# A smaller ordering margin, summed weights for a node's own messages, and two full matmuls for the targets' terms

## The chip, the cores and the metric

The kernel runs on one core of one Trainium2 chip. The metric is the device time of one execution in microseconds; the time before is the median of three runs, 4530.78 us (4525.29 to 4530.98). A profile is one more execution with the hardware profiler on. Engines are called PE (TensorE matmul), PEld (its weight loads), DVE (VectorE), ACT (ScalarE), POOL (GpSimd) and SP (which issues the DMAs).

## The reference

64 graphs of 256 nodes with 128 features pass through four residual graph layers (a graph convolution, a hyperbolic one, one with messages per edge, and a four-step dense one). All is fp32. The adjacency matrices are sparse: about 3% of the entries beside the diagonal are not zero, and the diagonal is full. The change touches only layer 2, whose core is:

```python
m_j = einsum('bnd,do->bno', node_features, W1[:D])      # sources
m_i = einsum('bnd,do->bno', node_features, W1[D:])      # targets
pre = m_j[:, None, :, :] + m_i[:, :, None, :] + b1
msg = gelu(layernorm(pre, g1, be1))                     # exact
agg = einsum('bijo,bij->bio', msg, adjacency)
updated = layernorm(concat([node_features, agg]) @ W2 + b2, g2, be2)
```

A message from a node to itself has both terms from the same node: `h @ W1[:D] + h @ W1[D:] + b1`. That equals `h @ (W1[:D] + W1[D:]) + b1`.

## The kernel before, in words

**Edges in lanes.** A graph's adjacency is cut into 8 blocks of 32 targets by 3 blocks of 86 sources, 24 blocks. The edges of a block (without the diagonal) are packed into 128 lanes. `g.hot` holds for each block a matrix with two ones for every lane: one at the row of its source (rows 0 to 85) and one at the row of its target (rows 96 to 127). One matmul of `hot` with a `table` that has the sources' terms in rows 0 to 85 and the targets' terms in rows 96 to 127 therefore gives the sum of both for all lanes of the block.

**Layer 2** (line 1039). After a layer norm, a ReLU and a transpose, `hT` (features by nodes, 128x256) is the input of four pieces which run side by side (`together`, line 1101):

- `sources` (line 1057): three matmuls with `w1[:, 0, :]` into one PSUM bank, the bias added by DVE into `a`, then four copies on POOL into `table[:86]`, two for the first four target blocks and two for the rest.
- `targets(0)` and `targets(1)` (line 1086): each makes four matmuls, one for 32 targets, all with output partitions 96 to 127 of a bank of its own, waits in the plan until the previous graph has left the stage of messages, and has ACT copy the bank, repeated for three source blocks, into `table[96:, c*4:(c+1)*4]`.
- `diagonal` (line 1046): for each half of the nodes two accumulating matmuls with the two parts of `w1` give the own messages' terms, DVE adds the bias into `mown`, and `messages` (line 1017) makes norm and GELU of them.

Then come six blocks of messages (`block_sums`, line 1106): four `table,hot` matmuls into a bank of the pool `psm`, squares on ACT (`junk`, with the sum in `sq`), a reciprocal root on POOL (`sq`), scale on DVE (`msg`), an offset on POOL, the GELU on ACT, and four matmuls into `pagg`, whose four outputs lie in four groups of 32 partitions. There is one `table` and one `pagg`, so a graph can fill the table only when the one before has left this stage.

**PSUM.** Five banks (`ps`) serve nearly everything, two (`psm`) the message blocks, one is `pagg`.

**Order.** Each layer of each graph is a generator that issues an instruction or a few and yields. `run` (line 1228) keeps several graphs alive and decides who goes next. A planner (`Clock`, line 60) adds an assumed duration to every issued instruction, knows when each engine and each tile will be free, and so gives each live generator a time at which its next instruction could begin. Of those whose time lies within a margin of the earliest, the one with the lowest graph number is taken. The order so found is kept word for word (`keep_in_program_order`, line 177, the line under which nearly all instructions appear in the profile), and each engine works through its part of it in order. A change of an assumed duration, of the number of pieces or of the margin therefore moves instructions of the whole program. The planner counts a matmul with an output of at most 32 columns of weights as a quarter of a full one.

**ACT's function tables.** Exp and Ln need one table, GELU and Tanh another; the planner puts an `ACT_TABLE_LOAD` (line 106) wherever its order changes between them.

Of the kernel before, what the change touches and what calls it, by code (L numbers as in the profile page):

```python
# [10 lines left out]
ALU = mybir.AluOpType  # L11
# [4 lines left out]
P = 128  # L16
N = 256
NC = N // P
D = 128
# [7 lines left out]
CAP = 128  # L27
TB = 4
TE = 6
MSGS = 4  # L30

LN_EPS = 1e-5
# [149 lines left out]
class Sparse:  # L182
# [142 lines left out]
    def setup(self):  # L325
        nc, w = self.nc, self.w
        self.ident = self.c("ident", [P, P])
        make_identity(nc, self.ident)
        self.ones = self.full("ones", [P, P], 1.0)
        self.half = self.full("half", [P, 2 * NC], 0.5)  # L330
        self.mhalf = self.full("mhalf", [P, NT], -0.5)

        self.w0 = self.matrix("w0", w["L0_gnn_W"])
        self.b0 = self.row("b0", w["L0_gnn_b"])

        self.attw = self.c("attw", [P, 2])
        self.column(None, w["L1_gnn_att_w"][D : 2 * D], self.attw[:, 0:1])
        self.column(None, w["L1_gnn_att_w"][0:D], self.attw[:, 1:2])
        self.attb = self.row("attb", w["L1_gnn_att_b"])

        self.w1 = self.matrix("w1", w["L2_gnn_W1"])
        wsum = self.c("wsum", [P, 2])
        nc.vector.tensor_reduce(wsum, self.w1, AX.X, ALU.add)
        nc.vector.tensor_scalar_mul(wsum, wsum, 1.0 / D)
        for k in range(2):
            nc.vector.tensor_scalar(self.w1[:, k, :], self.w1[:, k, :], wsum[:, k : k + 1], None, ALU.subtract)
        self.b1 = self.row("b1", w["L2_gnn_b1"])
        bsum = self.c("bsum", [P, 1])  # L350
        nc.vector.tensor_reduce(bsum, self.b1, AX.X, ALU.add)
        nc.vector.tensor_scalar_mul(bsum, bsum, -1.0 / D)
        nc.vector.tensor_scalar(self.b1, self.b1, bsum[:, 0:1], None, ALU.add)

        self.g1 = self.row("g1", w["L2_gnn_g1"])
        nc.vector.tensor_scalar_mul(self.g1, self.g1, float(D) ** 0.5)
        self.be1 = self.row("be1", w["L2_gnn_be1"])
        self.w2 = self.matrix("w2", w["L2_gnn_W2"])
        self.b2 = self.row("b2", w["L2_gnn_b2"])
        self.g2 = self.row("g2", w["L2_gnn_g2"])  # L360
        self.be2 = self.row("be2", w["L2_gnn_be2"])
        self.setup_layer3()
        self.setup_lanes()
# [675 lines left out]
    def layer2(self, n, g):  # L1039
# [6 lines left out]
        def diagonal():  # L1046
            po = yield from self.bank(self.ps, (P, NC, D))
            for c in range(NC):
                self.mm(po[:, c, :], [(hT[:, c * P : (c + 1) * P], self.w1[:, k, :]) for k in range(2)])
            yield  # L1050
            nc.vector.tensor_tensor(own, po, self.over(self.b1, NC), ALU.add)
            yield
            self.close(self.ps)
            yield
            yield from self.messages(own, own, NC)

        def sources():

            pa = yield from self.bank(self.ps, (P, NJB, D))
            for j in range(NJB):  # L1060
                w = self.width(j)
                self.mm(pa[:w, j, :], [(hT[:, j * JB : j * JB + w], self.w1[:, 0, :])])
            yield
            a = self.t("a", [P, NJB, D], bufs=1)
            w = self.width(NJB - 1)
            b1 = self.over(self.b1, NJB)
            nc.vector.tensor_tensor(a[:JB, : NJB - 1], pa[:JB, : NJB - 1], b1[:JB, : NJB - 1], ALU.add)
            yield
            nc.vector.tensor_tensor(a[:w, NJB - 1], pa[:w, NJB - 1], self.b1[:w], ALU.add)
            yield  # L1070
            self.close(self.ps)
            while self.left["messages"] < n:
                yield
            self.clock.since(self.when.get(("messages", n - 1), 0.0))
            yield
            for c in range(NC):
                rows = slice(c * NQ, (c + 1) * NQ)
                for js, k in ((slice(0, NJB - 1), JB), (slice(NJB - 1, NJB), w)):
                    near = a[:k, js].rearrange("p (o j) d -> p o (j d)", o=1)
                    nc.gpsimd.tensor_copy(  # L1080
                        table[:k, rows, js].rearrange("p i j d -> p i (j d)"),
                        near.to_broadcast([k, NQ, near.shape[2]]),
                    )
                    yield

        def targets(c):
            pc = yield from self.bank(self.ps, (P, NQ, D))
            for q in range(NQ):
                i = c * NQ + q
                self.mm(pc[P - IB :, q, :], [(hT[:, i * IB : (i + 1) * IB], self.w1[:, 1, :])])  # L1090
            yield
            while self.left["messages"] < n:
                yield
            self.clock.since(self.when.get(("messages", n - 1), 0.0))
            far = pc[P - IB :].rearrange("p q (o d) -> p q o d", o=1).to_broadcast([IB, NQ, NJB, D])
            nc.scalar.copy(table[P - IB :, c * NQ : (c + 1) * NQ], far)
            yield
            self.close(self.ps)
            yield

        yield from self.together(n, [sources(), targets(0), targets(1), diagonal()])
        yield from self.enter(n, "layer2", "messages")
        g.sums = 0
        pagg = self.psa.tile([P, NC, D], F32, tag="pagg", name="pagg")
# [123 lines left out]
    def run(self, x, adj, out, B):  # L1228


        def point(one):

            at = []
            while hasattr(one, "gi_frame") and one.gi_frame:
                at.append((one.gi_code.co_name, one.gi_frame.f_lineno))
                one = one.gi_yieldfrom
            return tuple(at)

        first = {}
        layers = {  # L1240
            "load": (lambda n, g: self.load(n, g, x, adj, out), "load"),
            "adjacency": (self.adjacency, "adjacency"),
            "scaled": (self.scaled, "scaled"),
            "layer0": (self.layer0, "layer0"),
            "lanes": (self.lanes, "hot"),
            "layer1": (self.layer1, "map"),
            "layer2": (self.layer2, "update"),
            "layer3": (self.layer3, "end"),
        }

        self.behind = {
            "load": [("pairs", 5), ("scaled", 5), ("layer0", 2)],
            "adjacency": [("load", 0), ("layer0", 2), ("scaled", 3)],
            "scaled": [("adjacency", 0), ("end", 2)],
            "layer0": [("adjacency", 0), ("map", 3)],
            "lanes": [("load", 0), ("ball", 3)],
            "hot": [("messages", 3)],
            "layer1": [("layer0", 0), ("pairs", 2), ("map", 3)],
            "pairs": [("hot", 0), ("messages", 3)],
            "ball": [],  # L1260
            "map": [("update", 3)],
            "layer2": [("map", 0), ("update", 2)],
            "messages": [],
            "update": [("end", 2)],
            "layer3": [("update", 0), ("scaled", 0)],
            "end": [],
        }
        graphs = [Graph() for _ in range(B)]
        clock = self.clock
        self.left = dict.fromkeys(self.behind, 0)  # L1270
        self.when = {}
        begun = dict.fromkeys(layers, 0)
        live = self.live = []
        while self.left["end"] < B:
            for name, (layer, last) in layers.items():
                n = begun[name]
                if n < B and self.ready(n, name):
                    live.append([self.at(n, name), n, name, layer(n, graphs[n]), last])
                    begun[name] += 1

            points = [point(one[3]) for one in live]
            begin = [max(one[0], clock.free.get(first.get(p), 0.0)) for one, p in zip(live, points)]
            soon = min(begin) + 0.2
            k = min((k for k in range(len(live)) if begin[k] <= soon), key=lambda k: (live[k][1], begin[k]))
            one = live[k]
            clock.now = clock.end = one[0]
            clock.first = None
            over = next(one[3], live) is live
            if clock.first:
                first[points[k]] = clock.first  # L1290
            one[0] = max(clock.end, one[0] + 0.1)
            if over:
                clock.end = one[0]
                live.remove(one)
                if one[4]:
                    self.leave(one[1], one[4])
# [614 lines left out]
```

## Time and profile before

| what | value |
|---|---|
| median of three runs | 4530.78 us |
| the profiled execution | 4534.37 us, of which the span from first to last instruction is 4532.6 |
| mean granted PE clock | 0.838 of full speed |
| ACT_TABLE_LOAD | 376 loads, 482.4 us of ACT, 1283 ns each |
| DVE `hot<-bank,lane` | 512 instructions, 266.5 us |
| POOL `ersn<-ew,mhalf` (a power of 24 columns) | 64 instructions, 271.1 us, 4236 ns each |

The page gives each engine's busy time and its share of the span, the span in 40 slices, the chain of work that ended last (followed back from the last instruction, at each step to what released it) and the costliest groups of instructions. A group is written as `output<-inputs`, its shape, its count, its busy time, the mean of one in ns, and the engine's idle time just before it with what ended that. All PSUM banks are called `bank`; the weights `w0`, `w1` and `w2` all appear as `w`. A matmul's shape `128*32 128x128` means 128 rows by 32 columns of weights and a moving operand of 128 by 128. Over the 64 graphs the span gives about 71 us a graph, while a graph is under way for several times as long: three to four are in the program at any time.

### The profile page before, as it was taken

The numbers are of one execution on the slowest core, as the hardware profiler recorded it, in microseconds if no ns is written. First come the engines' busy times: TensorE is split into PE (matmuls) and PEld (weight loads), VectorE is DVE, ScalarE is ACT, GpSimd is POOL, SyncE is SP. The second block draws the span as 40 slices with busy tenths as digits, with TensorE's granted clock in tenths as the row PEclk, the third lists the DMA queues.
The fourth block names the chain that finished last, engine by engine and source line by source line (L and its number), as shares of the span: only waits on it lengthen the run. The fifth ranks groups of instructions, "written<-read, shape, count | busy, mean of one in ns | idle before, by whom it ended". The sixth has DMA issues, their size and how long they took to land.

```text
span 4532.6 us, 85967 instructions
## 1 busy us (share of the span) xinstructions
PE 3624.9 (80%) x29143; PEld 3001.5 (66%) x29143; DVE 3154.1 (70%) x11739; ACT 2441.3 (54%) x7801; POOL 2831.3 (62%) x4945
## 2 busy tenths in 40 slices
PE   6688888778878878888787867888688888787876
PEld 5567666666767666666676656677576766676664
DVE  8666776677767767877676767767677677767652
ACT  2546555455556555655455455565555565655542
POOL 3666666576566666666566575665666666666653
PEclk7788878888888888888898878888887888888887
DMA  1000000000000000000000000000000000000000
GB/s 47 6 7 9 7 10 9 10 7 9 7 11 10 7 10 9 7 11 10 6 11 9 10 6 10 7 9 10 7 9 7 9 7 10 10 9 7 3 3 4
DMA packets 61585, 42.16 MB, mean 9 GB/s; under 512 B 6096, under 2 KB 61136, under 8 KB 61136
## 3 DMA queue, kind: packets, MB, share of 16 engines
q1 hardware_dynamic: 61136, 36.59, 2.9%
q8 instruction: 231, 3.78, 0.3%
q14 instruction: 218, 1.79, 0.1%
HBM read 28.19 MB, written 8.39 MB: 8 GB/s over the span
## 4 chain that ended last, share of the span: by engine, by line
PE 41%; DVE 24%; POOL 21%; ACT 8%; issue 5%; DMA 0%; SPq 0%; POOLq 0%; DVEq 0%; ACTq 0%
PE bank L177 40%; POOL sq L177 5%; POOL msg L177 4%; DVE msg L177 3%; POOL ersn L177 3%; POOL lnrs L177 2%; DVE hot L177 2%; ACT junk L177 2%; ACT L106 2%; DVE agg L177 2%; DVE src L177 1%; PE pagg L177 1%; DVE x2o L177 1%; DVE lnst L177 1%; ACT msg L177 1%
## 5 line engine op out<-in xcount | busy, mean ns | idle before, releaser
L177 DVE SCALAR_TENSOR_TENSOR msg<-bank,sq,g 128x128 f32<-128x128 f32 x1536 | 449.0, 343 | 271.7 <-POOL sq L177 256.9
L177 POOL TENSOR_TENSOR msg<-msg,be 128x512 f32<-128x512 f32 x384 | 490.3, 1281 | 173.2 <-DVE msg L177 134.9
L177 PE MATMUL bank<-table,hot 128*128 128x128 f32 x3072 | 459.4, 300 | 133.8 <-DVE msg L177 124.7
L177 PEld LDWEIGHTS bank<-table,hot 128*128 128x128 f32 x3072 | 420.9, 210 | 175.5 <-issue 49.7
L177 ACT ACTIVATE junk<-bank 128x128 f32<-128x128 f32 x1536 | 409.2, 278 | 189.9 <-PE bank L177 187.8
L106 ACT ACT_TABLE_LOAD x376 | 482.4, 1283 | 6.6
L177 POOL TENSOR_TENSOR sq<-sq,mhalf 128x4 f32<-128x4 f32 (+1 forms) x448 | 449.1, 1002 | 37.3
L177 PE MATMUL bank<-entries,hot 128*128 128x69 f32 x3072 | 443.8, 307 | 7.6 <-ACT entries L177 5.2
L177 PEld LDWEIGHTS bank<-entries,hot 128*128 128x128 f32 x3072 | 433.7, 224 | 24.4 <-issue 9.8
L177 PE MATMUL bank<-w,hT 128*128 128x128 f32 (+3 forms) x2432 | 417.0, 320 | 35.6 <-ACT hT L177 16.9
L177 PEld LDWEIGHTS bank<-w,hT 128*128 128x128 f32 (+3 forms) x2432 | 344.0, 178 | 99.9 <-issue 29.4
L177 ACT ACTIVATE msg<-msg 128x512 f32<-128x512 f32 x384 | 240.5, 628 | 250.1 <-POOL msg L177 241.1
L177 PE MATMUL bank<-wsd,f 128*128 128x256 f32 x1280 | 332.4, 391 | 35.3 <-ACT f L177 30.2
L177 ACT ACTIVATION_READ_ACCUMULATOR junk<-bank 128x1 f32 x1536 | 319.2, 208 | 0.1
L177 DVE TENSOR_TENSOR sd<-bank,bsd 128x512 f32<-128x512 f32 x256 | 175.9, 687 | 205.4 <-PE bank L177 203.8
L177 POOL TENSOR_SCALAR sq<-sq 128x4 f32<-128x4 f32 (+1 forms) x448 | 108.0, 241 | 331.9 <-ACT junk L177 304.2
L177 ACT ACTIVATE h<-x,lnnb,lnrs 128x128 f32<-128x128 f32 x384 | 175.8, 491 | 251.8 <-DVE lnnb L177 250.9
L177 PE MATMUL pagg<-msg,wgt 128*32 128x128 f32 x3072 | 174.5, 312 | 159.8 <-ACT msg L177 157.7
L177 PEld LDWEIGHTS bank<-wsd,f 128*128 128x128 f32 x1280 | 229.8, 191 | 77.0 <-ACT f L177 44.4
L177 DVE TENSOR_TENSOR hot<-bank,lane 128x384 f32<-128x384 f32 x512 | 266.5, 546 | 18.3 <-PE bank L177 17.5
L177 POOL TENSOR_TENSOR ersn<-ew,mhalf 128x24 f32<-128x24 f32 x64 | 271.1, 4236 | 4.1
L177 POOL COPY table<-a 86x1024 f32<-86x1024 f32 (+1 forms) x256 | 216.7, 875 | 88.3 <-DVE a L177 88.0
(261 smaller groups left out, 9593.1 us busy)
## 6 DMA issues: line engine op xcount, KB each, us to landing
adj<-in_adj_dram SPq DMA_DIRECT2D x64, 256.0 KB, 2.8
x<-in_x_dram SPq DMA_DIRECT2D x64, 128.0 KB, 2.1
out_dram<-xo SPq DMA_DIRECT2D x64, 128.0 KB, 1.9
wu<-in_L_gnn_wu_dram SPq DMA_DIRECT2D x4, 192.0 KB, 3.2
w<-in_L_gnn_W_dram SPq DMA_DIRECT2D x2, 128.0 KB, 3.9
b<-in_L_gnn_b_dram SPq DMA_DIRECT2D x3, 64.0 KB, 3.4
raw<-in_L_gnn_ws_dram SPq DMA_DIRECT2D x1, 192.0 KB, 2.4
raw<-in_L_gnn_wd_dram SPq DMA_DIRECT2D x1, 192.0 KB, 2.7
```

Of the source, the lines that this page charges most:

```text
L106: self.tc.keep_in_program_order(self.nc.scalar.preload_act_table_set(self.set))
L177: return c.tc.keep_in_program_order(f(*args, **kw))
```

## The change

Four edits. Weights: the set-up also makes `w1own`, the sum of the two parts of `w1`. `diagonal` uses it, with one matmul for each half of the nodes. `targets` is one piece: two matmuls with all 128 nodes of a half give the targets' terms in one bank, with each group of 32 targets in its own 32 partitions; four copies on ACT then take each group to partitions 96 to 127, and each fills one target block of both halves (`q::NQ`). In `run` the margin is 0.05 us of the plan instead of 0.2. Three new constants are used nowhere.

```diff
+GAPL, GAPM, GAPE = 1, 2, 3
...
         self.be1 = self.row("be1", w["L2_gnn_be1"])
+        self.w1own = self.c("w1own", [P, D])
+        nc.vector.tensor_tensor(self.w1own, self.w1[:, 0, :], self.w1[:, 1, :], ALU.add)
...
             for c in range(NC):
-                self.mm(po[:, c, :], [(hT[:, c * P : (c + 1) * P], self.w1[:, k, :]) for k in range(2)])
+                self.mm(po[:, c, :], [(hT[:, c * P : (c + 1) * P], self.w1own)])
...
-        def targets(c):
-            pc = yield from self.bank(self.ps, (P, NQ, D))
-            for q in range(NQ):
-                i = c * NQ + q
-                self.mm(pc[P - IB :, q, :], [(hT[:, i * IB : (i + 1) * IB], self.w1[:, 1, :])])
+        def targets():
+            pc = yield from self.bank(self.ps, (P, NC, D))
+            for c in range(NC):
+                self.mm(pc[:, c, :], [(hT[:, c * P : (c + 1) * P], self.w1[:, 1, :])])
             yield
             while self.left["messages"] < n:
                 yield
             self.clock.since(self.when.get(("messages", n - 1), 0.0))
-            far = pc[P - IB :].rearrange("p q (o d) -> p q o d", o=1).to_broadcast([IB, NQ, NJB, D])
-            nc.scalar.copy(table[P - IB :, c * NQ : (c + 1) * NQ], far)
-            yield
+            for q in range(NQ):
+                far = pc[q * IB : (q + 1) * IB].rearrange("p c (o d) -> p c o d", o=1).to_broadcast([IB, NC, NJB, D])
+                nc.scalar.copy(table[P - IB :, q::NQ], far)
+                yield
             self.close(self.ps)
             yield

-        yield from self.together(n, [sources(), targets(0), targets(1), diagonal()])
+        yield from self.together(n, [sources(), targets(), diagonal()])
...
-            soon = min(begin) + 0.2
+            soon = min(begin) + 0.05
```

## The prediction

> **What bounds the kernel now.** I read the page first (busy shares, then the chain that ended last), then the groups of instructions with shapes kept apart, then the waits, and last the timeline and the chain in a few windows around the stage that the change touches.
>
> ```profile
> span 4532.6 us, 85967 instructions
> PE 3624.9 (80%) x29143; PEld 3001.5 (66%) x29143; DVE 3154.1 (70%) x11739; ACT 2441.3 (54%) x7801; POOL 2831.3 (62%) x4945
> PE 41%; DVE 24%; POOL 21%; ACT 8%; issue 5%; DMA 0%; SPq 0%; POOLq 0%; DVEq 0%; ACTq 0%
> ```
>
> No engine is full. PE is the busiest and has the largest share of the chain, but the other engines together have more: the program is many short dependent steps of three to four graphs laid over each other, and PE is the queue in which most of them meet. A microsecond taken from PE is worth something only where PE was late. The rows that carry the change (columns: busy us, mean ns of one | idle before):
>
> ```profile
> L177 PE MATMUL bank<-w,hT 128*128 128x128 f32 x1024 | 195.6, 319 | 24.4 <-ACT hT L177 14.6 <-DVE hot L177 6.0 <-DVE prod L177 1.2
> L177 PE MATMUL pagg<-msg,wgt 128*32 128x128 f32 x3072 | 174.5, 312 | 159.8 <-ACT msg L177 157.7
> L177 PE MATMUL bank<-w,hT 128*32 128x128 f32 x1024 | 153.1, 309 | 6.6 <-DVE a L177 3.9 <-ACT table L177 1.5 <-ACT tgt L177 0.7
> L177 ACT COPY table<-bank 32x1536 f32<-32x1536 f32 x128 | 179.3, 1431 | 119.0 <-PE bank L177 118.5
> L177 ACT COPY binv<-bank 128x512 f32<-128x512 f32 x64 | 37.7, 589 | 21.8 <-PE bank L177 21.6
> ```
>
> The count tells how an fp32 matmul is recorded: the targets' 8 narrow calls per graph make 512 calls and 1024 records, so two records a call. The means overlap, so I divide busy time by records: 153.1/1024 = 150 ns for a narrow record, 195.6/1024 = 191 ns for a full one. A narrow one uses a quarter of the array and costs about as much. Compare `pagg`, also 32 wide: 174.5/3072 = 57 ns, because its four calls go to four different partition groups.
>
> Now the place (columns: start us, us, engine, line, operation) and, below it, one piece of the chain:
>
> ```profile
> 2038.30 2.98 PE L177 MATMUL bank<-w,hT 128*86 128x128 f32 x14
> 2043.57 2.15 PE L177 MATMUL bank<-w,hT 128*32 128x128 f32 x16
> 2053.62 1.05 PE L177 MATMUL bank<-table,hot 128*128 128x128 f32 x8
> ```
> ```profile
> 2035.04 10.69 PE bank L177 x54
> ```
>
> The burst of 16 narrow records takes 2.15 us (the commonest value of 19 such whole bursts in the timeline), and the chain runs through it without a gap: the 10.69 us piece covers it. I laid all PE pieces of the chain beside the rows of layer 2's first matmuls over the whole span: of 288 us of rows that begin with a narrow form, 224 us (78%) are on the chain. Who waits for them:
>
> ```profile
> ACT table L177 <- PE bank L177: 118.5, 71, 4.8
> POOL table L177 <- DVE a L177: 88.0, 41, 7.7
> DVE mown L177 <- PE bank L177: 82.2, 49, 4.8
> ```
>
> But what follows isn't tight: over the 64 graphs the first `table,hot` matmul starts 7.7 us (median) after the last ACT copy into the table and 6.4 us after the last POOL copy (6 graphs of 64 have under 1.8 us after ACT's), and from a graph's aggregate to the next graph's first table write 21 us pass (3 graphs under 5). The single table and the single `pagg` bank do not bind.
>
> **What the Trainium skill says.** "TensorE: Matmul & The Clock Gate", Part 3, says that narrow matmuls run side by side only if each has its own group of output partitions. The trace agrees: 57 ns with four groups, 150 ns for the targets, all of which write partitions 96 to 127. "TensorEngine Tiling (Array Packing)", Key Properties, says that a change of tiling mode drains the array. No row isolates that drain; but the order of the two built programs has 1733 changes between full, 32-column and 32-row forms before and 1577 after, so this can only help. "ScalarE: Activation LUTs", What ACT_TABLE_LOAD costs, gives about 1283 ns for a load; the page's row has 1283. The clock page, Part 1, has the array at half or full rate by its recent activity; here the mean granted clock is 0.838, slices 0.7 to 0.9, which fits a mixture.
>
> **The change part by part.** The order of both built programs gives the counts.
>
> (1) Targets. Out go 512 narrow calls (1024 records), in come 128 full ones (256 records, at 191 ns 48.9 us). By the rows: 153.1 - 48.9 = 104 us of PE. By bursts: 2.15 us becomes a burst of 4 records, 0.71 us for the median 4-record row of this form, so 1.44 x 64 = 92 us.
>
> (2) A node's own messages. 256 calls become 128: 256 records fewer, 48.9 us by the row; by bursts 1.05 (8 records) - 0.71 = 0.34, times 64 = 22 us. Together PE loses 114 to 153 us, 3 to 4% of its 3625; I take the middle of the two sums, rounded to 135. The weights' sum is one more DVE instruction in the set-up, under a microsecond, beside waits for weight loads.
>
> (3) On the path: 78% of 135 is 105 us. When PE is earlier, something else is next: POOL's copies into the table, which depend on the sources' matmuls ahead of the narrow burst and end 1.3 us after ACT's in the median. That side isn't shortened by (1), except where PE's queue is earlier as a whole. I keep four fifths: 84 us. Bounds: the 114 to 153 us in full above, 40 below (rival B).
>
> (4) ACT's copies. Two of 32x1536 (1431 ns) become four of 32x768. The slope from `binv` (512 wide, 589) to 1536 wide is (1431-589)/1024 = 0.82 ns an element, so 768 wide is about 800 ns (an estimate): 3.20 for 2.86 us, 0.34 x 64 = 22 us of ACT. In the new order the four are interleaved: from first to last table copy there are 6.0 places on ACT instead of 1.4, and what stands between is mostly the own messages' squares (99 times), which followed anyway, with 22 table loads. Each copy now spans both halves of the table, so the first message block needs all four instead of the first: at most 3.20 - 1.43 = 1.8 us later. The 7.7 us of slack hides that in 58 of 64 graphs; 6 x 1.8 = 11 us where it doesn't. What is queued behind a waiting copy on ACT (squares, hT copies, tanh) is delayed by its 0.34 us. The whole program has 393 table loads for 383: 10 x 1.283 = 13 us. ACT's 22 + 13 = 35 us count by its share: 8% of the chain for 54% busy, so 15% of it, 5 us. With half of the 11 exposed: about 10 us. Bounds 0 and 46.
>
> (5) One PSUM bank instead of two is held from the targets' matmuls until the copies. The pool has five. PE waits on `table` for a bank for 9.2 us in all: gain 0 to 9, taken as 0.
>
> (6) The margin, 0.2 to 0.05. It issues no new work, but the whole order changes: SP keeps its 365 instructions and DMA is 3% busy, so the loads do not matter; POOL keeps 4977. PE's runs of equal instructions stay at 11279; DVE's go from 9925 to 10666, that is, graphs are interleaved more finely there. From ranks to update a graph is spread over 3.67 graphs' worth of PE instructions instead of 3.50: more overlap, which feeds waiting engines, and more instructions of younger graphs ahead of older ones. Nothing in the trace of before prices this. I bound it at 1% (45 us) either side, and take 0.
>
> Sum: -84 + 10 = -74. The profiled execution took 4534.4 us for a span of 4532.6, 3.6 above the median of 4530.8; from the median, 4530.8 - 74 = about 4457, -1.6%.
>
> **The rivals.** A, the forecast: 4457, its own range 4405 to 4500.
>
> B, PE's relief is mostly absorbed. For it: the 6.4 to 7.7 us before the first `table,hot` say that the table's filling is seldom last, POOL ends after ACT, and 59% of the chain isn't PE. Against: 78% of these rows lie on the chain and ACT stood idle 118.5 us for them. It gives about 40 us, less 10: 4501.
>
> C, slower. The place is DVE's queue, 24% of the chain: 741 more breaks of runs, each of which can put one instruction of a younger graph (3154.1/11739 = 269 ns) ahead of an older one whose step everything else waits for. All of them: 199 us. It cancels the 74 us from 275 breaks on. By DVE's share of the chain (24% for 70% busy, a third) it is 68 us, short of that; at two thirds it is 133 - 74 = +59: 4590. For it: message blocks also grow in the PE order (from first `hot` to last `pagg` 131 instructions before, 140 after). Against: the 21 us of slack between graphs swallow such delays, and POOL's order, with the longest single instructions (`ersn`, 4236 ns), has `ersn` inside a message stage in 3 graphs after and 2 before.
>
> D, the change doesn't do what it says: excluded for the counts, which stand in the built program; the margin could be without effect, but the order shows that it isn't.
>
> **How the numbers follow.** Chances: A 0.57, B 0.20, C 0.21, a larger gain below 4385 0.02. Predicted is A's time. The range needs A and B whole and about a third of C: 4385 (the full 153 us, little else, and nothing lost) to 4560. It contains a clock change too: 0.01 of granted clock is 1.2% of PE's 3480 us, 41 us of PE, half of it on the chain. This kernel's measurement tells 0.2% (9 us) from nothing. Faster by more than that: A and nearly all of B, 0.75. Within it: the edge between B and C, 0.05. Slower: 0.20.
>
> **What would show it.** Right: the narrow row gone, PE busy near 3480 us, `ACT table <- PE bank` well below 118.5, PE's share of the chain lower, a group of 256 copies near 800 ns. For B: `POOL table <- DVE a` and PE's idle time grow by what PE's busy time lost. For C: DVE's and POOL's shares of the chain grow, with `DVE msg <- POOL sq` and `PE pagg <- ACT msg` longer. I am wrong if the order costs or gains more than 45 us, which nothing in the trace of before excludes firmly.

## The result, and the profile after

The changed kernel takes 4450.0 us (median of 4 runs, 4440.4 to 4453.8) against 4528.0 us of the kernel before in the same session: a ratio of 0.9825, 95% interval 0.9806 to 0.9843, or 79 us of 4531 (the medians differ by 78). The prediction said 4457. The profiled execution took 4440.4 us, at the lower end of its runs, so its span of 4438.6 shows a little more than the median gain.

From the page of the changed kernel: the span, the busy time of each engine, and the chain by engine.

```profile
span 4438.6 us, 84015 instructions
PE 3575.3 (81%) x28119; PEld 2964.4 (67%) x28119; DVE 3050.9 (69%) x11740; ACT 2484.0 (56%) x7939; POOL 2837.7 (64%) x4945
PE 36%; DVE 29%; POOL 21%; ACT 9%; issue 5%; DMA 0%; SPq 0%; POOLq 0%; DVEq 0%; ACTq 0%
```

PE has 1024 records fewer, as counted, and its share of the chain fell from 41% to 36%. But its busy time fell by 50 us only, not by 135. The groups with shapes kept apart tell why (busy us, mean ns of one | idle before; the first line is of the kernel before, the others of the changed kernel):

```profile
L177 PE MATMUL bank<-entries,hot 128*128 128x69 f32 x3072 | 443.8, 307 | 7.6 <-ACT entries L177 5.2
L178 PE MATMUL bank<-entries,hot 128*128 128x69 f32 x3072 | 492.7, 329 | 14.1 <-ACT entries L178 12.3 <-ACT aggT L178 1.1
L178 PE MATMUL bank<-w,hT 128*128 128x128 f32 x768 | 174.9, 348 | 7.9 <-ACT hT L178 2.8 <-ACT aggT L178 2.2 <-DVE hot L178 1.6
L178 PE MATMUL bank<-w1own,hT 128*128 128x128 f32 x256 | 48.3, 321 | 3.5 <-DVE hot L178 3.5
```
```profile
L178 ACT COPY table<-bank 32x768 f32<-32x768 f32 x256 | 201.9, 789 | 82.8 <-PE bank L178 78.2
```

The narrow row of 153.1 us is gone and the two full rows together hold 223.2 us where one held 195.6. Work that nobody touched became dearer: `entries,hot` went from 443.8 to 492.7 us with the same 3072 records. Two things are in that. The mean granted clock fell from 0.838 to 0.819 (0.813 to 0.819 in the four runs); but most of the rise of this row comes with the new order, since the kernel with the smaller margin alone (e1 below) already has 480.0 us in it at a clock of 0.843. ACT's copies cost 789 ns, 22.6 us more in all.

The waits for the stage's matmuls became shorter (us, times, longest):

```profile
ACT table L178 <- PE bank L178: 78.2, 47, 5.1
POOL table L178 <- DVE a L178: 57.5, 40, 5.9
DVE mown L178 <- PE bank L178: 14.7, 14, 2.5
```

Not all of that is the shorter burst. With the old order kept (e11 below) the first falls from 118.5 to 67.4 us and the third from 82.2 to 18.6, but the second stays near its 88.0 (83.2): it fell by the new order.

### The profile page after: what moved, and what is told of

Its sections match the earlier page's. It is cut to its first block, busy times and chain, and to the rows that moved or that the text cites. A ratio compares the mean times of both kernels' runs of the same rounds, so it can differ in the third digit from the quotient of the medians.

```text
span 4438.6 us, 84015 instructions
## 1 busy us (share of the span) xinstructions
PE 3575.3 (81%) x28119; PEld 2964.4 (67%) x28119; DVE 3050.9 (69%) x11740; ACT 2484.0 (56%) x7939; POOL 2837.7 (64%) x4945
## 4 chain that ended last, share of the span: by engine, by line
PE 36%; DVE 29%; POOL 21%; ACT 9%; issue 5%; DMA 0%; SPq 0%; POOLq 0%; DVEq 0%; ACTq 0%
PE bank L178 34%; POOL sq L178 4%; POOL msg L178 3%; POOL lnrs L178 3%; DVE msg L178 3%; POOL ersn L178 2%; DVE hot L178 2%; DVE src L178 2%; ACT L107 2%; DVE agg L178 2%; PE pagg L178 1%; ACT junk L178 1%; DVE lnst L178 1%; DVE pos L178 1%; DVE x2o L178 1%
## 5 line engine op out<-in xcount | busy, mean ns | idle before, releaser
L178 PE MATMUL bank<-entries,hot 128*128 128x69 f32 x3072 | 492.7, 329 | 14.1 <-ACT entries L178 12.3
L178 PEld LDWEIGHTS bank<-entries,hot 128*128 128x128 f32 x3072 | 482.1, 246 | 31.6 <-ACT entries L178 16.4
L178 PE MATMUL bank<-table,hot 128*128 128x128 f32 x3072 | 434.0, 288 | 35.4 <-DVE msg L178 26.9
L178 PEld LDWEIGHTS bank<-table,hot 128*128 128x128 f32 x3072 | 399.1, 199 | 75.2 <-DVE msg L178 27.1
L178 PE MATMUL bank<-wsd,f 128*128 128x256 f32 x1280 | 346.0, 403 | 72.9 <-ACT f L178 61.1
L178 PE MATMUL pagg<-msg,wgt 128*32 128x128 f32 x3072 | 171.6, 304 | 179.9 <-ACT msg L178 179.1
L178 PE MATMUL bank<-adjn,sd 128*128 128x256 f32 x768 | 268.7, 435 | 51.9 <-DVE sd L178 51.8
L178 PE MATMUL bank<-ident,h 128*128 128x128 f32 x512 | 153.3, 383 | 168.1 <-ACT h L178 147.9
```

Source lines behind the costliest of these rows:

```text
L178: return c.tc.keep_in_program_order(f(*args, **kw))
```

## The experiments

Two questions follow: how much of the 79 us is the work that was removed, and how much is the new order that the planner makes of changed work and a changed margin. All ratios are against the kernel before, run on the same chip in the same session; a ratio times 4531 gives the us. Where two experiments of different sessions are compared, the difference is that of their ratios.

**The edits one by one.** Each is a part of the change's diff, the rest left as before.

> The kernel before with the margin 0.05 alone. If the gain came from the PE work removed (theory W): no change beyond what another order does by chance, 4528 within 45 us. If it came from the order (theory O): about 4450, nearly the whole 78 us.

```diff
-            soon = min(begin) + 0.2
+            soon = min(begin) + 0.05
```

Measured (e1): 4409.8 us, ratio 0.9724 (0.9700 to 0.9748). The margin alone gains 125 us, more than the whole change.

> The kernel before with the summed weights for the own messages alone, margin 0.2. W: 256 records fewer, 22 to 49 us of PE of which about 0.62 shows: 4498 to 4515. O: 4528.

```diff
-                self.mm(po[:, c, :], [(hT[:, c * P : (c + 1) * P], self.w1[:, k, :]) for k in range(2)])
+                self.mm(po[:, c, :], [(hT[:, c * P : (c + 1) * P], self.w1own)])
```

Measured (e2): 4474.4 us, 0.9866 (0.9842 to 0.9889), a gain of 61 us: more than the 22 to 49 us of PE work that it removes, so something else must be in it.

> The kernel before with the targets' full matmuls and four copies alone, margin 0.2. W: 92 to 104 us of PE less, about 0.62 of it shows, 10 us of ACT lost: about 4475. O: 4528, or up to 4540 by the copies.

Measured with the new `targets` alone (e3): 4563.2 us, 1.0063 (1.0038 to 1.0087): 28 us slower, though it takes the narrow matmuls away and also made 26 table loads fewer.

> The changed kernel with the margin back at 0.2, so both matmul edits and no change of margin. W: about 4455, within the changed kernel's own noise of another order. O: about 4528.

Measured (e4): 4512.3 us, 0.9952 (0.9938 to 0.9967). So with both matmul edits in place the margin is worth 0.9825/0.9952, or 1.3%, half of what it is worth alone. The single edits, -125, -61 and +28 us, do not add up to -79, and neither theory as I had stated them fits: every edit also makes the planner draw up another order for the whole program. Work and order had to be separated.

**The order kept, work put back.** In the next two, matmuls are issued that the plan does not count, so that the order on ACT, DVE and POOL is the changed kernel's instruction by instruction, and PE only has the additional ones in it.

> The changed kernel, its order kept on every engine, with the eight narrow targets' matmuls of each graph put back on PE as dead work that the plan does not count (the full ones overwrite them). They were 153 us of PE. If PE work on the path is worth 0.62 of itself (W): +95, about 4545. If PE is hidden here (O, or the rival of an absorbed gain): +25 or less, about 4450 to 4475.

```diff
             pc = yield from self.bank(self.ps, (P, NC, D))
+            for i in range(NIB):
+                self.unplanned(pc[P - IB :, i % NC, :], [(hT[:, i * IB : (i + 1) * IB], self.w1[:, 1, :])])
```

Measured (e5): 4504.2 us, 0.9934 (0.9918 to 0.9951), 49 us above the changed kernel's 0.9825. The dead row is 157.0 us, PE's busy time rose by 107 us to 3681.9, and the clock rose to 0.829 to 0.831. So the narrow work was on the path, but only a third of its own time showed; both theories of the expectation missed.

> The changed kernel, its order kept, with the own messages' matmul done twice (the second overwrites the first; the plan counts one). 256 records, 22 to 49 us of PE. W: +14 to +30, 4464 to 4480. O: within 9 us of 4450.

```diff
             for c in range(NC):
+                self.unplanned(po[:, c, :], [(hT[:, c * P : (c + 1) * P], self.w1own)])
+            for c in range(NC):
                 self.mm(po[:, c, :], [(hT[:, c * P : (c + 1) * P], self.w1own)])
```

Measured (e6): 4456.0 us, 0.9829 (0.9812 to 0.9846), not to be told from the changed kernel's 0.9825: 2 us, where the intervals leave room for about 13, for 31 us more of PE's busy time. The own messages' second matmul is worth little or nothing in this order. If that holds in the order of e2 as well, which no run tried, nearly all that e2 gained was its new order.

**The order kept, work exchanged.** Here the planner is told of the old instructions and the new ones are issued in their places: two full matmuls where it counted the first four narrow ones, none for the other four, two copies where it counted one.

> The kernel with margin 0.05 alone (4410 us), its order kept on every engine: the plan still counts narrow matmuls and two copies, while two full matmuls and four copies are issued in their places. Theory R: the targets' work is a gain by itself, 0.35 (what the dead narrow work cost) of 104 us, and the edit loses by the order that the planner makes of it: about 4375. Theory X: the work itself loses, by the copies that all have to be done before the first message block or by a lower clock: 4435 to 4450.

```diff
-                self.mm(pc[P - IB :, q, :], [(hT[:, i * IB : (i + 1) * IB], self.w1[:, 1, :])])
+                args = dict(lhsT=hT[:, i * IB : (i + 1) * IB], rhs=self.w1[:, 1, :])
+                clock.end = max(clock.end, clock.took("tensor", "matmul", (pc[P - IB :, q, :],), args))
+            banks.append(pc)
+            if len(banks) == 1:
+                for e in range(NC):
+                    self.unplanned(pc[:, e, :], [(hT[:, e * P : (e + 1) * P], self.w1[:, 1, :])])
...
```

Measured (e7): 4382.0 us, 0.9658 (0.9642 to 0.9674), 30 us below the margin alone (e1). Theory R holds: the targets' work is a gain by itself in this order. That the edit lost in e3, with the margin 0.2, because of the order made of it, is borne out by the next run, which keeps the order of that margin.

> The kernel before with both matmul edits issued in the places that its own plan gives to the old instructions: margin 0.2 and the old order on every engine. What the work alone is worth. By the prediction's sum: -74, about 4460. By what the kept orders showed so far (28 us for the targets, 6 us for the own messages): about 4500. If a lower clock gives it all back: 4530.

Measured, with both matmul edits in the old order with the old margin (e11): 4496.1 us, 0.9916 (0.9899 to 0.9932). This is the change's work alone: 38 us of 4531 (31 to 46), half of the 74 that the prediction gave it. It is the cleanest run to read, since each engine has the same order as before. Where the planner makes its own order of the same two edits (e4, 0.9952), 16 us of this are lost. Two lines of its page, and the row of one form of matmul that did not change, in the kernel before and here:

```profile
span 4489.5 us, 84060 instructions
PE 3542.4 (79%) x28119; PEld 2938.1 (65%) x28119; DVE 3150.4 (70%) x11740; ACT 2458.4 (55%) x7929; POOL 2824.7 (63%) x4945
```
```profile
L177 PE MATMUL bank<-adjc,sd 128*128 128x256 f32 x768 | 238.4, 393 | 0.0
L177 PE MATMUL bank<-adjc,sd 128*128 128x256 f32 x768 | 248.0, 407 | 0.0
```

and its timeline where layer 2 begins:

```profile
2017.54 1.49 PE L177 MATMUL bank<-w,hT 128*86 128x128 f32 x6
2018.82 1.06 PE L266 MATMUL bank<-w,hT 128*128 128x128 f32 x4
2022.10 0.61 PE L266 MATMUL bank<-w1own,hT 128*128 128x128 f32 x4
2032.89 1.05 PE L177 MATMUL bank<-table,hot 128*128 128x128 f32 x8
```

The burst of 2.15 us has become 1.06 in this place. PE's busy time fell by 82.5 us (3624.9 to 3542.4), where the rows of the exchanged matmuls alone would give 130; most of the rest went into matmuls such as `adjc,sd`, at a clock of 0.819 to 0.823 instead of 0.831 to 0.838. That this is the clock can be read off the trace, in which the granted clock is either full or half at any moment. An `adjc,sd` record lasts 379 ns on average at the full clock and 601 to 609 at half, in both kernels; of the 768 records, 48 fell into half-clock stretches before and 93 do here, which accounts for the 9.6 us of the row. A stretch of each kind from e11 (length, then busy us and instructions of PE, PEld, DVE, ACT and POOL, the granted clock, DMA), and a group of the row in each:

```profile
2020.40:2022.00 1.60, 1.60 (x9) 1.42 (x8) 1.53 (x5) 1.57 (x3) 0.74 (x2) 1.00 0.00 0
2027.80:2030.20 2.40, 2.40 (x7) 1.84 (x6) 2.17 (x12) 1.61 (x2) 1.80 (x5) 0.50 0.00 0
2020.81 0.59 PE L177 MATMUL bank<-adjc,sd 128*128 128x256 f32 x2
2029.43 1.06 PE L177 MATMUL bank<-adjc,sd 128*128 128x256 f32 x2
```

**Do the orders add up, and is it the margin?**

> The kernel before with the margin 0.05 and the summed weights, without the targets' edit. If the edits add up: 4410 - 58 = about 4352. If single orders differ by chance and the own messages' work is worth only the 6 us that its doubling cost: 4404, within 45.

Measured (e8): 4429.5 us, 0.9755 (0.9739 to 0.9772): 14 us slower than the margin alone, only just outside the noise of the two. An edit that gained 61 us in one plan gains nothing in another, which fits the second theory.

> The kernel before with the margin 0.1. If the time depends on the margin itself: between the two, 4440 to 4500. If one order is as good as another by chance: anywhere between 4400 and 4560, also outside the two.

> The kernel before with the margin 0. If the time depends on the margin itself: at or below 4420. If by chance: anywhere between 4400 and 4560.

```diff
-            soon = min(begin) + 0.2
+            soon = min(begin) + 0.1
```

Measured: 4515.6 us, 0.9948 (0.9932 to 0.9965) with 0.1 (e9, the edit above), and 4463.7 us, 0.9834 (0.9818 to 0.9851) with 0 in its place (e10). Both lie outside what was expected if the time followed the margin. A smaller margin was faster than 0.2 at all three values, but the times are not in order: 0.05 is 50 us better than 0. Three values can't tell a best margin from a good draw.

Taken with the other runs, though, the margins fall into two groups. In the orders that the planner makes for the work that is issued, the ratio is 0.9724 to 0.9834 with a margin of 0.05 or 0 (e1, e8, e10 and the changed kernel), and 0.9866 to 1.0063 with 0.1 or 0.2 (e2, e3, e4, e9 and the kernel before): every order of the first group is faster than every order of the second, whatever the edits. The traces divide in the same way. With the small margins, 9330 to 9434 DVE instructions begin before the one ahead of them on DVE has ended, and DVE is busy for 3045 to 3063 us; with the large ones it is 8537 to 8634 instructions and 3143 to 3170 us. A number in the planner fits this step: it counts DVE as free 0.082 us before an instruction's result is there (`return ends - 0.082, ends`). A margin above 0.082 lets the oldest graph go on with a step that needs this result; a margin below it puts a ready step of another graph in between. No run changes that number, so the reading is not tested, and two orders of one group still differ by up to 50 us (e1, e10) or 89 (e2, e3).

Where an order gains is seen in what PE waited for. From the waits of PE in e1:

```profile
PE pagg L177 <- ACT msg L177: 117.4, 82, 5.2
PE bank L177 <- DVE hot L177: 85.8, 112, 4.3
PE bank L177 <- DVE msg L177: 59.1, 50, 8.0
```

In the kernel before these were:

```profile
PE pagg L177 <- ACT msg L177: 157.7, 109, 7.7
PE bank L177 <- DVE hot L177: 134.7, 110, 8.9
PE bank L177 <- DVE msg L177: 124.7, 63, 14.6
```

These three alone shrank by 155 us, while PE's work stayed (3632.1 us for 3624.9). PE's idle time, span less busy, went from 908 to 779 us, as much as the span lost and a little more. Two of the three are waits for a message block on its way through DVE, POOL and ACT; it fits that with the smaller margin PE more often has another graph's matmuls to do meanwhile. It is not what every faster order shows: in the changed kernel `PE pagg <- ACT msg` is 179.1 us, more than before.

> The same in the order of the kernel with margin 0.05 alone (4410 us): the run of the targets' work in that order, 4382, with the summed weights in place. If the own messages' work is worth 6 us: about 4376. If it is worth what the edit alone gained (58 us): about 4325. If the gain of that order is tied to the old work: above 4410.

Measured (e12): 4380.7 us, 0.9659 (0.9643 to 0.9676), the same as e7 (0.9658). The own messages' matmul is worth nothing that can be measured here either, though PE's busy time fell by 26 us (3556.6 to 3531.0). In the program, what is made of its result is needed only when the message blocks are done. This kernel has the change's own work, with its margin, in the order that the planner makes for the old work: 1.7% below the changed kernel (0.9659/0.9825). With e7 it is the fastest kernel of the study.

## Why the prediction was right, and where its sum was not

The time was met within 7 us, but that is luck: two terms were off in opposite directions. Against the kernel before, the work gave -38 us (e11), and the order gave the rest: 0.9825/0.9916, or 42 us (30 to 53). The prediction had -74 and 0.

- Steps (1) and (2), the PE time removed: 135 us predicted. By the rows of e11 it is 130 (153.1 out, 195.6 become 171.9 + 46.7). Right. Its two halves are not worth the same: the own messages' share showed no measurable gain in either kept order (e6, e12).
- Step (3), "I keep four fifths: 84 us": the mis-sized term. First, 130 us of rows took only 82.5 us from PE, for the most part since a lower clock made the other matmuls dearer; the prediction had the clock only as a widening of its range. Second, of these 82.5 us some 38 showed, 46%. The 78% read from the chain says how often the burst was last, not what is left when it is shorter. PE's share of the chain over its share of busy time, 41/80 or 51%, a ratio which the prediction used for ACT and DVE but not here, would have come nearer. e5 gives 46% too (49 us of time for 107 of PE) and e7 40% (30 for 75.5). But this is a fit after the fact, and it fails for the own messages: 31 us of PE were worth 2 us in e6, 26 were worth nothing beyond noise in e12.
- Step (4), the copies: 800 ns and 22 us predicted, 789 ns and 22.6 us measured, ten table loads more on the page (386 for 376). What they cost in time was not tried by itself; it is contained in e7's and e11's gains.
- Step (5), the bank held for less long, was not tried by itself.
- Step (6), "I bound it at 1% (45 us) either side, and take 0": wrong as a bound. The margin is worth 125 us alone and 1.3% with the matmul edits in place. A new order moved the time by about -59 us in e2, if its work is worth the 2 us of e6, by +14 in e8 against e1, by +16 in e4 against e11, and by some +58 for the targets (e3's +28 less e7's -30, two different orders). In the sum of this change the order came to -42, at the edge of the bound; e1's, e2's and the targets' orders lie well outside it.
- Rival B, 40 us less 10 for the copies, came near the work's gain of 38, but its cause is not seen: with the old order `POOL table <- DVE a` didn't grow (88.0 before, 83.2 in e11). PE's idle time did, by 39 us (908 to 947), but that is about half of the 82.5 us of PE's busy time that went, not all of it. Rival C, slower by more breaks on DVE, did not occur: a DVE share of 29% of the chain for 24% is what it said to look for, but `PE pagg <- ACT msg` and `DVE msg <- POOL sq` grew by 21 and 23 us only, and the order was a gain. "PE busy near 3480" as a sign was wrong: 3575.

Which property makes one order better than another is left open, beyond PE's waits and the two groups of margins. The prediction had read the finer order on DVE from the built programs and priced it as a risk only, in rival C. DVE's busy time is some 100 us lower in the finer orders (3057 in e1, 3051 in the changed kernel, 3154 before) with the same instructions, but for one in the set-up of the changed kernel. In e1, 55 of the 97 us are more overlap of neighbouring instructions (the sum of their durations exceeds the busy time by 742 us for 687); the other 42 are shorter durations. What these 97 us are worth in time is open.

## What to carry to other kernels

Where a planner puts the whole program in order, every edit is two: the work, and another order. Measure the work with the order kept, by telling the planner of the old instructions; otherwise an edit that removes work can look slower (e3), and one whose work is worth little can look like a large gain (e2). For work taken from a busy but not full engine, first subtract what the clock takes back. Here some 40 to 46% of what was left showed for the targets, near the engine's share of the chain over its share of busy time (51%), and next to nothing for a result that is needed late.

## What the runs showed of the hardware

**Removing narrow matmuls lowered PE's clock.** In three pairs with the same order the kernel without them had a mean granted clock lower by 0.010 to 0.015: 0.819 to 0.823 for 0.831 to 0.840 (e11 and the kernel before, beside it and in the other sessions), 0.831 to 0.835 for 0.843 to 0.844 (e7 and e1), 0.813 to 0.819 for 0.829 to 0.831 (the changed kernel and e5). "TensorE: Matmul & The Clock Gate", Part 1, of the Trainium skill ties the rate to recent activity of the array; the direction agrees. Taking out 256 full records moved it less: 0.828 to 0.831 for 0.831 to 0.835 (e12 and e7), and not visibly for the changed kernel and e6 (0.813 to 0.819, 0.815 to 0.819). That narrow matmuls count as activity for as long as they take is a reading that no run here isolates.

**A short DVE instruction can last as long as a POOL instruction beside it.** From the timeline of the changed kernel (start, us):

```profile
689.21 1.48 POOL L178 TENSOR_TENSOR ow<-wgt,ev 128x768 f32<-128x768 f32 x1 [2.27 <-DVE ev L178]
689.53 1.19 DVE L178 TENSOR_TENSOR most<-most,at 128x6 f32<-128x6 f32 x1
```

The DVE instruction has a median of 0.16 us; here it takes 1.19 and ends 0.03 us after POOL's. "SBUF — State Buffer", SBUF: two separate sides, says that a DVE instruction with two SBUF inputs and a POOL instruction that reads SBUF exclude each other for a whole instruction, which fits this case. In the kernel before, 288 DVE instructions took over 0.4 us more than the median of their group (same operation, tiles and shape), 243 us together, and 262 of them (91%) ended within 0.25 us of the end of a POOL instruction, where 41% of all DVE instructions do. In the changed kernel they were 301, with 225 us, so this does not explain the change.
